# Second-layer row terms of a two-layer graph and expert kernel: broadcast by a trip through DRAM instead of by TensorE

## The chip, the cores and the metric

The kernel runs on one core of a Trainium2 chip. The metric is device time in microseconds (us) of one execution. In the text PE is TensorE (PEld its weight loads), DVE is VectorE, ACT is ScalarE, POOL is GpSimd, and SP is the sync engine, which here only issues DMAs. L525 is line 525 of the kernel before.

## What is computed

The input x holds 64 independent graphs ("batches") of 256 nodes with 256 features; all share one 256x256 adjacency matrix. Two layers follow each other, each a graph attention and a feed-forward part. The change touches the attention of the second layer:

```
h = layernorm(x) @ W                     # L1_gnn
e_src, e_dst = h @ a[:256], h @ a[256:]
e = leaky_relu(e_src[:, :, None] + e_dst[:, None, :], 0.01)
e = where(adj == 0, -1e9, e)
x = x + relu(softmax(e, -1) @ h)
```

Its feed-forward part sends every node to two of eight experts (256 to 256 to 256, with gelu) and adds the weighted results.

## The kernel before

**Work and order.** Each batch of 256 rows is two tiles of 128 rows. The function `batch_layers` is a generator for one batch: it records some instructions and then yields a number. The main loop at the end of the kernel runs in steps; three steps (TICKS) after one batch a new one begins, so that about seven batches are in flight. In a step every live generator runs once, in the order of the numbers they yielded (a lower number first); a positive number ends the generator's turn until the next step, a negative one puts it back into the same step with that rank. The order so recorded is the order of each engine's instructions; every engine and every DMA queue works strictly in its order. Expert work (`expert_pair`, pairs of 128 rows of one expert) is put between the batches' pieces by the same ranks.

**The second layer's scores.** After exponentials, leaky_relu turns into a maximum: for a target node j and a source node i the unnormalised weight is me[j, i] times max(term[i], own[j]). `projected1` (L513) has ACT write three numbers per node into the small tile `ex`: a factor that goes into the masked matrix `me` (L519), the row term, and the node's own term. The row terms lie one to a partition, but the scores need all 256 of them along the free axis in every partition. `scores1` makes this with two PE transposes of a broadcast column (L525) into a PSUM bank named `pd`, and then DVE computes the two halves of the score tile `z1` (L530) with `scalar_tensor_tensor`. `z1` has one buffer, 128 x 2 x 256 float32. In a later step `attended` (L586) multiplies `z1` with the projected nodes on PE (the 128x257 form of that line), and ACT takes out the result (L690).

**The first layer does the same by DMA.** From batch 1 on, `send_terms` (L539) collects the first layer's terms with a DVE transpose, a 4 KB DMA writes them to DRAM (L623), and a second DMA, `spread_terms` (L556), reads them into all 128 partitions of the last part of the score tile `z4`, 512 KB. From batch 18 (SETTLED) on both are issued on SP, before that on ACT.

**SP's queue.** In a step in the middle SP issues, in this order: the first layer's terms to DRAM (L623, waits for DVE), the next batch's input (L96, 256 KB, named `xin`), the spread of the terms (L556, waits until L623 has landed), the store of an earlier batch's result (L736), then for two expert pairs the rows (L893, four DMAs), the row tails (L904) and the weights (L922), and the next batch's blocks (L106, four DMAs).

PSUM is eight banks used in turn (tag "bank"), whatever they hold. POOL sends rows to the experts' regions (L1061) and adds expert results to the output (L991) by indirect DMAs.

Of the kernel before, what the change touches and what calls it, by code (L numbers as in the profile page):

```python
# [9 lines left out]
F32 = mybir.dt.float32  # L10
I32 = mybir.dt.int32
AF = mybir.ActivationFunctionType
ALU = mybir.AluOpType
AX = mybir.AxisListType

P = 128
# [5 lines left out]
def rows_to_all(ap: bass.AP, n: int) -> bass.AP:  # L22

    return bass.AP(tensor=ap.tensor, offset=ap.offset, ap=[[0, P], [1, n]])
# [3 lines left out]
def kernel(  # L28
# [17 lines left out]
    nc = tc.nc  # L46
    B, N, D = x.shape
# [4 lines left out]
    NT = N // P  # L52
# [21 lines left out]
    work = ctx.enter_context(tc.tile_pool(name="work", bufs=2))  # L74
# [4 lines left out]
    def bank(name, shape):  # L79
        t = psum.tile([P, 2 * D], F32, tag="bank", name=name, bufs=8)  # L80
        n = 1
        for s in shape:
            n *= s
        t = t[:, :n]
        if len(shape) == 2:
            t = t.rearrange("p (a b) -> p a b", a=shape[0])
        elif len(shape) == 3:
            t = t.rearrange("p (a b c) -> p a b c", a=shape[0], b=shape[1])
        return t
# [39 lines left out]
    SETTLED = CHUNKS[0] + CHUNKS[1] + CHUNKS[2] + CHUNKS[3] + 2  # L129


    ident = const.tile([P, P], F32, tag="ident", name="ident")
# [191 lines left out]
    def once(work):  # L324
# [14 lines left out]
        out=tri, in_=tri, pattern=[[1, P]], base=0, channel_multiplier=-1,  # L339
# [154 lines left out]
    for i in range(2):  # L494
        t = keep.tile([P, NT, D + 1], F32, tag=f"q1_{i}", name=f"q1_{i}")
# [3 lines left out]
    def projected1(xT, rstd, b):  # L499

        q = q1s[b % 2]
        pqs = []
        for t in range(NT):
            pq = bank("pq", [D + 3])
            for k in range(KT):
                nc.tensor.matmul(  # L506
                    pq, xT[:, k, t * P : (t + 1) * P], wx1[:, k, :],
                    start=(k == 0), stop=(k == KT - 1),
                )
            pqs.append(pq)  # L510
        ex = small.tile([P, NT, 3], F32, tag="ex1", name="ex1")
        for t, pq in enumerate(pqs):
            nc.scalar.activation(ex[:, t, :], pq[:, D:], AF.Exp, scale=rstd[:, t : t + 1])  # L513
            nc.scalar.activation(
                q[:, t, :D], pq[:, :D], AF.Copy, scale=rstd[:, t : t + 1]
            )
        me = work.tile([P, NT, N], F32, tag="me", name="me", bufs=1)
        for j in range(NT):
            nc.scalar.activation(me[:, j, :], masks[1][:, j, :], AF.Copy, scale=ex[:, j, 0:1])  # L519
        return q, ex, me  # L520

    def scores1(ex, me):
        pd = bank("pd", [N])
        for t in range(NT):
            nc.tensor.transpose(  # L525
                pd[:, t * P : (t + 1) * P], ex[:, t, 1:2].to_broadcast([P, P]), ident
            )
        z = work.tile([P, NT, N], F32, tag="z1", name="z1", bufs=1)
        for j in range(NT):
            nc.vector.scalar_tensor_tensor(  # L530
                z[:, j, :], pd, ex[:, j, 2:3], me[:, j, :], op0=ALU.max, op1=ALU.mult
            )
        return [z[:, j, :] for j in range(NT)]

    def send_terms(q, b):


        ut = small.tile([P, S], F32, tag="ut", name="ut", bufs=1)
        nc.vector.transpose(  # L539
            ut.rearrange("p (t h w) -> p t h w", t=NT, h=H), q[:, :, :, HD - 1 : HD + 3]  # L540
        )
        ud = tc.dram_tile([S, S], F32, name=f"terms_{b}")
        ud = ud.rearrange("c r -> (c r)").rearrange("(c p) -> c p", p=P)
        return ut, ud
# [51 lines left out]
    def batch_layers(b, c0, xng, lg):  # L596
# [23 lines left out]
        if b:  # L620
            ut, ud = send_terms(q, b)
            yield -31
            terms_queue(b).dma_start(  # L623
                out=ud.rearrange("c (g r) -> g c r", g=G),
                in_=ut[2 : P : S // (NT * H), :],
            )
            yield -52
        z = work.tile([P, NT, NT, H, P], F32, tag="z4", name="z4", bufs=2)
# [17 lines left out]
        ex = work.tile([P, NT, D], F32, tag="e", name="e", bufs=1)  # L646
# [21 lines left out]
        for t in range(NT):  # L668
            nc.vector.scalar_tensor_tensor(  # L669
                x2[:, t, :], pf[:, t, :], rstd[:, t : t + 1], x1b[:, t, :],  # L670
                op0=ALU.mult, op1=ALU.add, accum_out=sums[:, t : t + 1],
# [6 lines left out]
        xT = transposed(x2)  # L678
        yield 20
        q, ex, me = projected1(xT, rstd, b)  # L680
        yield 25
        z = scores1(ex, me)
        yield 40
        pvs, rinv = attended(
            q[:, :, None, :], 1, lambda j, h, t: z[j][:, t * P : (t + 1) * P]
# [9 lines left out]
        for t in range(NT):  # L695
            nc.vector.scalar_tensor_tensor(
                x2[:, t, :], x2[:, t, :], 1.0, rel[:, t, :],
                op0=ALU.mult, op1=ALU.add, accum_out=sums[:, t : t + 1],
# [36 lines left out]
        if not dense:  # L735
            d = nc.sync.dma_start(  # L736
                out=out_rows[b * N : (b + 1) * N, :].rearrange("(t p) d -> p t d", p=P), in_=base
# [476 lines left out]
    def jobs():  # L1214
        b = done = taken = 0
        for c, nb in enumerate(CHUNKS + (1,) * DENSE):
            nt = nb * NT
            lg = keep.tile([P, nt, E], F32, tag="lg", name=f"lg_{c}", bufs=7)
            xng = []
            row0 = b * N  # L1220
            done += nt
            n = max(done - (E - 1) - taken, 0) if b < ROUTED else 0
            taken += n
            for i in range(nb):
                def job(b=b, c=c, i=i, nb=nb, nt=nt, n=n, lg=lg, xng=xng, row0=row0):
                    yield from batch_layers(b, i * NT, xng, lg)
                    if i == nb - 1:
                        if b >= ROUTED:
                            yield 65
                            yield from route_dense(b, lg)  # L1230
                        else:
                            yield from route(c, row0, nt, n, b == ROUTED - 1, xng, lg)
                yield job()
                b += 1
# [85 lines left out]
```

## Time and profile before

| | us |
|---|---|
| median of 3 runs (1497.18 to 1500.99) | 1497.51 |
| the profiled execution, its own time | 1509.41 |
| its span, first to last instruction | 1507.6 |
| PE busy in the span | 1429.0 (95%) |
| DVE busy | 1252.7 (83%) |
| ACT busy | 1024.6 (68%) |
| POOL busy | 870.2 (58%) |

The span of the profiled execution is 1.8 us shorter than its own time, and that time is 11.9 us (0.8%) above the median of the runs; differences are therefore made against the profiled execution and then put onto the median. The mean granted clock of PE was 0.986. The span has three stretches: some 300 us in which the pipeline of batches fills and the first experts begin, a steady part up to about 1300 us with a new batch every 20.3 us, and an end of about 200 us in which only expert work is left. The row of L525 (128 transposes, 26.1 us busy) and that of L530 (128 instructions, 53.8 us busy) are those of the scores concerned.

### The profile page before, as it was taken

What the parts mean: (1) busy time and instruction counts of PE and PEld (TensorE: products, weight loads), DVE (VectorE), ACT (ScalarE), POOL (GpSimd) and SP (SyncE); (2) the same over time, 40 slices, a digit from 0 to 9 for tenths busy, and PEclk for the clock granted to TensorE, in tenths of its full rate; (3) what the DMA queues carried; (4) which work ended last, traced back from release to release, by engine and by line L of the source; (5) the groups of instructions that cost most, each with busy time, mean ns of one, the idle gap of its engine ahead of it and who ended that gap; (6) DMA issues with size and microseconds to landing.
All of it is one profiled execution on the core that took longest, in us unless ns stands there. A gap on an engine that the chain in (4) does not pass through costs nothing. (4 is left out here: it accounts for less than half of the span.)

```text
span 1507.6 us, 30029 instructions
## 1 busy us (share of the span) xinstructions
PE 1429.0 (95%) x8138; PEld 1263.9 (84%) x8138; DVE 1252.7 (83%) x4476; ACT 1024.6 (68%) x2403; POOL 870.2 (58%) x845
## 2 busy tenths in 40 slices
PE   6899999999999999999999999999999999879996
PEld 5788888889898998988998989888888887658885
DVE  7699999888898888889898988998888888765543
ACT  1477667577777777777777787667777878764331
POOL 2122536355867576666758585776666667643444
PEclk9899999899999999999999999999999999999999
DMA  4732334556877777877877677768777775887843
GB/s 134 241 97 67 117 104 131 155 149 142 196 172 190 157 183 155 177 177 180 187 157 183 151 186 164 181 164 187 179 167 170 153 170 124 192 180 161 156 83 50
DMA packets 354354, 236.37 MB, mean 157 GB/s; under 512 B 246276, under 2 KB 316428, under 8 KB 354188
## 3 DMA queue, kind: packets, MB, share of 16 engines
q1 hardware_dynamic: 301272, 158.16, 41.3%
q0 software_dynamic: 48864, 66.33, 23.8%
q10 hardware_dynamic: 4052, 9.98, 2.2%
q8 instruction: 67, 1.10, 0.3%
q14 instruction: 99, 0.81, 0.2%
HBM read 146.00 MB, written 88.35 MB: 155 GB/s over the span
## 5 line engine op out<-in xcount | busy, mean ns | idle before, releaser
L991 POOL DMA_INDIRECT out_dram<-y,xt x258 | 414.1, 1605 | 206.6 <-issue 71.5
L586 PE MATMUL pv<-q,z 128*128 128x65 f32 (+1 forms) x2560 | 365.9, 298 | 0.4
L586 PEld LDWEIGHTS pv<-q,z 128*128 128x128 f32 x2560 | 333.0, 194 | 13.1 <-DVE z L572 1.1
L1061 POOL DMA_INDIRECT xs<-xng,pos x244 | 259.5, 1064 | 65.3 <-issue 60.3
L970 PE MATMUL py<-w2s,hT 128*128 (+1 forms) x1224 | 283.5, 382 | 11.5 <-ACT hT L961 10.3
L970 PEld LDWEIGHTS py<-w2s,hT 128*128 128x128 f32 x1224 | 229.1, 191 | 45.4 <-ACT hT L961 14.2
L955 PE MATMUL ph<-sT,we 128*128 128x256 f32 x1032 | 241.9, 383 | 4.5 <-DVE y L980 2.9
L572 DVE SCALAR_TENSOR_TENSOR z<-z,q,mask 128x256 f32<-128x256 f32 x504 | 231.6, 482 | 15.5 <-DMA z<-terms 6.6
L955 PEld LDWEIGHTS ph<-sT,we 128*128 128x128 f32 x1032 | 195.6, 192 | 32.4 <-DVE y L980 3.6
L461 ACT COPY xT<-pt 128x512 f32<-128x512 f32 x209 | 121.4, 588 | 105.0 <-PE pt L455 72.2
L948 ACT ACTIVATE y<-y,w 128x256 f32<-128x256 f32 x258 | 113.2, 498 | 115.3 <-DVE y L980 100.9
L961 ACT ACTIVATE hT<-ph,we 128x256 f32<-128x256 f32 x306 | 124.1, 472 | 63.5 <-PE ph L955 46.3
L408 POOL TENSOR_SCALAR rstd<-mv 128x4 f32<-128x4 f32 (+1 forms) x66 | 15.6, 236 | 239.4 <-DVE mv L381 184.4
L506 PE MATMUL pq<-wx,xT 128*128 128x259 f32 x512 | 128.8, 394 | 18.6 <-ACT xT L461 16.9
L426 ACT ACTIVATE off<-x,sums 128x256 f32<-128x256 f32 x256 | 129.3, 505 | 8.4 <-DVE x L669 1.6
L506 PEld LDWEIGHTS pq<-wx,xT 128*128 128x128 f32 x512 | 95.6, 193 | 42.6 <-ACT xT L461 25.6
L471 PE MATMUL pq<-wx,xT 128*128 128x268 f32 x512 | 127.1, 391 | 2.8 <-DVE xT L117 1.6
L980 DVE TENSOR_TENSOR y<-py,b2s 128x512 f32<-128x512 f32 x129 | 85.7, 685 | 50.0 <-PE py L970 37.3
L662 PE MATMUL pf<-wfT,xT 128*128 128x256 f32 x512 | 123.8, 385 | 0.0
L471 PEld LDWEIGHTS pq<-wx,xT 128*128 128x128 f32 x512 | 97.5, 191 | 21.9 <-DVE xT L117 1.8
L690 ACT ACTIVATE rel<-pv,rinv 128x256 f32<-128x256 f32 x128 | 54.0, 469 | 76.4 <-DVE rinv L593 52.2
L662 PEld LDWEIGHTS pf<-wfT,xT 128*128 128x128 f32 x512 | 94.7, 195 | 10.8
(174 smaller groups left out, 2400.8 us busy)
## 6 DMA issues: line engine op xcount, KB each, us to landing
we<-wpack SPq DMA_DIRECT2D x145, 288.0 KB
xr<-xs SPq DMA_DIRECT2D x516, 64.0 KB
z<-terms SPq DMA_DIRECT2D x46, 512.0 KB
xin<-in_x_dram SPq DMA_DIRECT2D x64, 256.0 KB
out_dram<-base SPq DMA_DIRECT2D x61, 256.0 KB
xblk<-in_x_dram SPq DMA_DIRECT2D x188, 64.0 KB
z<-terms ACTq DMA_DIRECT2D x17, 512.0 KB
out_dram<-y,xt POOLq DMA_INDIRECT x258
```

Source lines behind the costliest of these rows:

```text
L426: nc.scalar.activation(off, src[:, t, :], AF.Square, bias=sums[:, t : t + 1], scale=-float(D), accum_out=sq[:, at + t : at + t + 1],)
L461: nc.scalar.copy(dst, pt)
L471: nc.tensor.matmul(pq.rearrange("p h c -> p (h c)"), xT[:, k, t * P : (t + 1) * P], wx[:, k, :], start=(k == 0), stop=(k == KT - 1),)
L506: nc.tensor.matmul(pq, xT[:, k, t * P : (t + 1) * P], wx1[:, k, :], start=(k == 0), stop=(k == KT - 1),)
L572: nc.vector.scalar_tensor_tensor(z[:, j, :, h, :], terms, q[:, j, h, HD + 2 : HD + 3], masks[0][:, j, :].rearrange("p (t i) -> p t i", t=N ...
L586: nc.tensor.matmul(pv[:, h, :], z(j, h, t), q[:, j, h, : d + 1], start=(j == 0), stop=(j == NT - 1),)
L662: nc.tensor.matmul(pf[:, t, :], xT[:, k, t * P : (t + 1) * P], wfT[:, k, :], start=(k == 0), stop=(k == KT - 1),)
L955: nc.tensor.matmul(ph[:, f, :], we[:, k * D + f * P : k * D + (f + 1) * P], xT[:, k, :], start=(k == 0), stop=(k == KT - 1),)
L961: nc.scalar.activation(hT[:, f, :], ph[:, f, :], AF.Gelu, bias=we[:, C_B1 + f : C_B1 + f + 1])
L970: nc.tensor.matmul(py[:, t, :], hT[:, f, t * P : (t + 1) * P], w2s[:, e, f * D : (f + 1) * D].rearrange("p e c -> p (e c)"), start=(f == 0 ...
L991: d = nc.gpsimd.indirect_dma_start(out=out_rows, out_offset=bass.IndirectOffsetOnAxis(ap=xt[:, t, 0:1].bitcast(I32), axis=0), in_=y[:, t, ...
L1061: d = nc.gpsimd.indirect_dma_start(out=xs_d[: E * CAP * PAIR, :], out_offset=bass.IndirectOffsetOnAxis(ap=at, axis=0), in_=xe, in_offset=None,
```

## The change

For batches 18 to 63 (46 of 64) the second layer's row terms no longer go over PE. In the step that computes `ex`, a DMA on SP writes the 256 terms out of `ex` into a DRAM tile (`send_terms1`, 256 pieces of 4 bytes); later in the same step a second DMA on SP reads them into all 128 partitions of the second half of `z1` (128 pieces of 1 KB, 128 KB). `scores1` takes its terms from there: the first half of the scores is written beside them, the second half over them. `z1` is therefore taken one step earlier than before. The rank of `scores1` in its step goes from 25 to 45. Batches 0 to 17 keep the transposes.

In the built program the order of DVE, ACT and POOL is unchanged; PE's is unchanged but for the 92 transposes that are gone; SP's is unchanged but for 92 DMAs that are added. In the middle of the program the write of the second layer's terms stands just ahead of L623, and the read just behind `xin` (L96) and just ahead of L556. For the last seven batches no `xin` stands between; for the last three, which have no first-layer terms beside them, the read stands right behind its write.

```diff
-    def scores1(ex, me):
-        pd = bank("pd", [N])
-        for t in range(NT):
-            nc.tensor.transpose(
-                pd[:, t * P : (t + 1) * P], ex[:, t, 1:2].to_broadcast([P, P]), ident
-            )
-        z = work.tile([P, NT, N], F32, tag="z1", name="z1", bufs=1)
+    def send_terms1(ex, b):
+
+        ud = tc.dram_tile([N], F32, name=f"terms1_{b}")
+        nc.sync.dma_start(out=ud.rearrange("(t p) -> p t", p=P), in_=ex[:, :, 1])
+        return ud
+
+    def scores1(ex, me, z, spread):
+
+        terms = z[:, NT - 1, :]
+        if not spread:
+            terms = bank("pd", [N])
+            for t in range(NT):
+                nc.tensor.transpose(
+                    terms[:, t * P : (t + 1) * P], ex[:, t, 1:2].to_broadcast([P, P]), ident
+                )
         for j in range(NT):
             nc.vector.scalar_tensor_tensor(
-                z[:, j, :], pd, ex[:, j, 2:3], me[:, j, :], op0=ALU.max, op1=ALU.mult
+                z[:, j, :], terms, ex[:, j, 2:3], me[:, j, :], op0=ALU.max, op1=ALU.mult
             )
...
         q, ex, me = projected1(xT, rstd, b)
-        yield 25
-        z = scores1(ex, me)
+        spread = b >= SETTLED
+        if spread:
+            yield -22
+            ud = send_terms1(ex, b)
+            yield -52
+        z = work.tile([P, NT, N], F32, tag="z1", name="z1", bufs=1)
+        if spread:
+            nc.sync.dma_start(out=z[:, NT - 1, :], in_=rows_to_all(ud, N))
+        yield 45 if spread else 25
+        z = scores1(ex, me, z, spread)
         yield 40
```

## The prediction

> **What bounds the kernel now.** I read the page's first part, then the busy times of stretches, then the timeline of one batch engine by engine, then PE's and SP's waits. PE leads, and the stretches say where:
>
> ```profile
> 320.00:960.00 640.00, 633.16 (x3739) 569.07 (x3738) 569.46 (x1968) 483.02 (x1142) 430.19 (x405) 1.00 0.75 172
> 960.00:1310.00 350.00, 328.40 (x1826) 287.83 (x1825) 302.15 (x1210) 271.41 (x590) 235.87 (x218) 0.98 0.76 167
> ```
>
> Columns: stretch and length, then busy us of PE, PEld, DVE, ACT, POOL, then clock, DMA share, GB/s. From 320 to 960 us (batches 18 to 48) PE is busy 99% of the time, DVE 89%. From 960 to 1310 (batches 49 to 63) PE is busy 94%, DVE 86%. PE's waits in the first stretch are 6.6 us of 640, for one cause:
>
> ```profile
> PE pq L506 <- ACT xT L461: 6.2, 8, 1.3
> PE pq L506 <- issue: 0.4, 1, 0.4
> ```
>
> So up to 960 us the end is PE's own work, and what PE issues less is saved. Later it is PE with some stalls (7.5 us there for DVE's x of L669, 6.9 us for ACT's xT).
>
> **What the Trainium skill says.** (1) "Perfetto Trace Analysis", Identifying the Most-Contended Engine: matmul busy time misleads because matmuls are pipelined. It does here: a transpose of L525 lasts 273 ns on the page, but PE goes on after 109. (2) "TensorE: Matmul & The Clock Gate", Part 4: a 128x128 transpose took about 275 ns in a kernel, most of it SBUF access latency; the 273 ns agree. (3) "DMA: Bandwidth & Descriptors", Anatomy of one DMA: about 2.0 us fixed, mostly the receipt of the write, plus bytes / 436 GB/s. The trace agrees: L556, which waits for L623 to land, is issued 2.24 us or less after it (below). (4) "VectorE: DVE Perf Modes", The TRN2 errata: a source in PSUM costs a DVE instruction 120 fixed cycles, one in SBUF 58. The trace does not: L572 from SBUF takes 483 ns (median), the 128x256 instructions from the PSUM bank 470 to 473. The measurement decides.
>
> **What is removed: 92 transposes.** The end of one batch's transposes in PE's timeline:
>
> ```profile
> 817.97 3.62 PE L970 MATMUL py<-w2s,hT 128*128 x16
> 821.42 0.38 PE L525 MATMUL pd<-ident,ex 128*128 128x128 f32 x2
> 821.64 1.56 PE L586 MATMUL pv<-q,z 128*128 128x65 f32 x13
> ```
>
> From start to start the two take 821.64 - 821.42 = 0.22 us; the 273 ns overlap with what follows. Batches 18 to 48: 31 x 0.22 = 6.8 us, with PE saturated, all on the path. Batches 49 to 63: 15 x 0.22 = 3.3 us, plus PE's waits for `ex` ahead of L525 and its weight load, 2.2 us in that stretch; I take half, 1.1, as what follows is sometimes late too. Sum 11.2 us; ends: 6.8 (nothing from the later stretch) and 12.3. The freed PSUM bank can only make later banks free earlier; I cost it at nothing, since PE shows no wait for a bank in the steady stretch.
>
> **What is added: two DMAs a batch on SP.** SP's timeline of the same batch, after ACT's `ex` and before DVE's scores (three views):
>
> ```profile
> 817.17 0.27 ACT L513 ACTIVATE ex<-pq,rstd 128x3 f32<-128x3 f32 x1
> ```
> ```profile
> 819.94 0.54 SPq L623 DMA_DIRECT2D terms<-ut  x1
> 820.52 0.45 SPq L96 DMA_DIRECT2D xin<-in_x_dram  x1
> 822.18 0.35 SPq L556 DMA_DIRECT2D z<-terms  x1
> ```
> ```profile
> 824.94 0.83 DVE L530 SCALAR_TENSOR_TENSOR z<-pd,ex,me 128x256 f32<-128x256 f32 x2
> 825.69 0.17 DVE L593 RECIPROCAL rinv<-pv 128x4 f32<-128x4 f32 x1
> 826.28 0.18 DVE L593 RECIPROCAL rinv<-pv 128x4 f32<-128x4 f32 x1 [0.42 <-PE pt L455]
> ```
>
> *The write.* It can go at 817.5, when `ex` is done; SP is idle there, since its next instruction, L623, waits for DVE until 819.94. Issue 0.39 (xt of L904, also 256 pieces) to 0.55 us (L623): hidden. Landing: like L623's, 1.7 to 2.2 us, as the lower end; no row shows 256 stores of 4 bytes, so 4 us as the upper. Thus landed at 819.2 to 821.5.
>
> *The read.* It stands behind xin, whose issue ends at 820.97, and ahead of L556, which waits until 822.18 anyway. It can go at 821.1 and takes some 0.35 us of issue: hidden in the 1.2 us. (With the slow write it goes at 821.5 and may hold L556 by a few tenths; L556's data are needed 8 us later or more, so that costs nothing.) Its buffer is free: the matmuls of the batch before that read `z1` were issued from 811.60 on, for 1.9 us. Landing: at least the fixed 2.0 plus 128 KB at 436 GB/s, 2.3 us. At most, with xin's 256 KB ahead: 393,000 bytes at 172 GB/s / 0.75 = 229 GB/s (the stretch's rate over its share), 1.7 us, so 3.7. (The fixed part and the 436 are estimates from the DMA page.) It lands at 823.4 to 824.8; I take 824.2. DVE wants it at 824.94, so it is on time by 0.1 to 1.5 us. Over the steady batches DVE gets to L530 3.1 to 4.3 us after the end of xin's issue; the shortest third may be late by some tenths. Behind L530 in DVE's order stand the reciprocals of L593, the product of L641 and x2 of L669, for which PE's transposes wait. But the second L593 waits for PE by 0.42 us here: that covers a small lateness. Cost up to 960 us: 0; upper end 31 x 0.3 = 9 us.
>
> *Later batches.* Here the margin is smaller. At 1058.12 xin is issued (0.45 us), at 1060.94 DVE reaches L530: 2.4 us instead of 3.1 to 4.3, and the same order holds for about ten batches. Against a landing of 2.3 to 3.7 us after 1058.7 DVE waits 0 to 1.4 us, say 0.6. PE is ahead of DVE there: it next needs DVE's x2 (finished at 1064.5) only after pl, issued from 1066.20 for 0.95 us. So I charge a third: 10 x 0.6 / 3 = 2 us; ends 0 and 14. For the last three the read follows its write directly, two landings (4 to 5 us) after `ex`: batch 61 has 4.4 us (1255.54 to 1259.96), the others more: a few tenths once. SP also stands still for 2 us there, behind which expert loads wait (batch 63: four us later than now); five row buffers are loaded ahead, cost 0, upper end 4.
>
> *SP itself.* 0.9 us more issue a batch. It waits long each batch ahead of L623:
>
> ```profile
> SPq L623 <- DVE stats L380: 343.7, 45, 11.4
> SPq L556 <- DMA terms<-ut: 41.1, 45, 2.2
> ```
>
> 343.7 / 45 = 7.6 us idle: hidden. *DMA engines:* 46 x 128 KB over some 1000 us are 6 GB/s beside 170, and 384 packets a batch: cost 0, as the queue's other loads have steps in hand; it is inside the landing's upper end. *DVE:* terms from SBUF, 483 - 470 = 13 ns x 92 = 1.2 us, hidden in the wait at L593. *Ranks:* 25 to 45 changes no engine's order.
>
> **Sum.** -11.2 + 2 = -9.2 us. The profiled time 1509.4 would become 1500.2, and the median, which stands 11.9 us lower, 1497.5 - 9.2 = 1488.3; I say 1488.
>
> **Rivals.**
> A. As summed, PE's issue time is what goes: 1485.5 to 1492. Chance 0.63. For it: PE at 99%.
> B. It all comes off, and earlier banks and fewer stalls give a little more: -13 or more, 1484.5. 0.11.
> C. The later part swallows it: only 6.8 us are saved, and ten or twelve late reads cost DVE, and through it PE, their full 0.6 us: 6.8 - 6.6 = about 0, 1494 to 1500. For it: DVE's gaps are few after 960 us. Against: PE's lead of 1 to 2 us over DVE there. 0.14.
> D. Slower: the read queued behind xin lands late in every batch. It decides from about 4.5 us after its issue on: margin 3 to 4 plus the 0.4 us of L593. At 5 us (L893's second group is let go only when L556's 512 KB have landed, some 5 us after their issue, so this length does occur) DVE stands 0.5 to 1 us in 46 batches: +23 to 46 us, less 11: 1509 to 1532. Against: 128 KB are a quarter of those 512. 0.09.
> E. A change without effect, the DMAs costing what PE saves by chance: within 0.3%, in C's range. 0.03.
>
> **How the numbers follow.** A measurement of this kernel tells some 0.3%, 4.5 us, from no change. Faster by more: A and B, and a small part of C: 0.76. Same: most of C and E: 0.14. Slower: D and the tail of C: 0.10. The range holds A, B and half of C: 1484 to 1498.
>
> **What would show it in the profile after.** 36 transposes of L525's kind instead of 128; PE's stretch of a batch 0.22 us shorter, the pace from 320 us on 20.1 instead of 20.3 us; DVE's wait for "z from terms", now 6.6 us in all, up by under 10 us, in the late batches; SP's wait ahead of the write short. I am wrong if DVE's wait for the terms grows beyond 20 us, if PE's idle time grows by what its work shrinks, or if expert loads come late at the end.

## The result and the profile after

| | before | after |
|---|---|---|
| median of 6 runs each, us | 1497.35 | 1822.76 |
| span of the profiled execution, us | 1507.6 | 1816.8 |
| PE busy, us | 1429.0 (95%) | 1527.7 (84%) |
| mean granted clock of PE | 0.986 | 0.910 |

The changed kernel is slower: ratio 1.217, 95% interval 1.214 to 1.220, some 325 us. The forecast of 1488 us was wrong in size and in sign.

In the kernel after, what was L530 is L538, L556 is L564, L623 is L631, L641 is L649, L647 is L655, L669 is L677. The new write is L525, the new read L696. The same stretches, cut so that they hold about the same batches as the two shown of before (columns as there):

```profile
320.00:1160.00 840.00, 695.42 (x3679) 605.08 (x3677) 571.70 (x1963) 483.18 (x1137) 428.65 (x406) 0.90 0.71 137
1160.00:1620.00 460.00, 360.70 (x1816) 313.57 (x1816) 307.12 (x1216) 273.31 (x595) 241.97 (x220) 0.87 0.67 129
```

In the first stretch DVE's 1963 instructions cost 572 us, as the 1968 of before did (569). But they take 840 us of time instead of 640: the work is the same, and 200 us of standing are added. PE was busy 99% and is now busy 83%, at a clock of 0.90 instead of 1.00. The waits of all engines (us in total, times, longest us) say who stands first:

```profile
DVE z L538 <- DMA z<-terms: 322.3, 46, 10.0
ACT e L655 <- DVE hp L649: 278.9, 44, 9.7
POOL rstd L446 <- ACT off L426: 240.8, 53, 11.2
...
PEld pt L455 <- DVE x L677: 213.1, 82, 9.8
PE pt L455 <- DVE x L677: 199.5, 55, 9.4
```

In the same list of before the four lower ones stood so (L641 and L669 are DVE's lines there):

```profile
POOL rstd L446 <- ACT off L426: 98.5, 33, 4.6
...
ACT e L647 <- DVE hp L641: 21.0, 30, 3.1
PEld pt L455 <- DVE x L669: 19.5, 28, 4.8
...
PE pt L455 <- DVE x L669: 13.4, 10, 4.4
```

Of the five after only DVE's is a wait for a DMA, in each of the 46 batches, 322.3 / 46 = 7.0 us each time. The growth of the others is what stands behind it: L649 and L677 come after L538 in DVE's order, and ACT's L426 works on the x of L677. The group row of L538 carries the same number (busy, mean ns of one, idle before it):

```profile
L538 DVE SCALAR_TENSOR_TENSOR z<-z,ex,me 128x256 f32<-128x256 f32 x92 | 44.6, 484 | 324.2 <-DMA z<-terms 322.3
```

Which of the two DMAs is late is in SP's timeline of one batch (start, duration, line), and in DVE's and PE's of the same time:

```profile
1003.47 0.38 SPq L525 DMA_DIRECT2D terms<-ex  x1
1005.95 0.55 SPq L631 DMA_DIRECT2D terms<-ut  x1
1006.55 1.87 SPq L96 DMA_DIRECT2D xin<-in_x_dram  x1
1012.53 0.34 SPq L696 DMA_DIRECT2D z<-terms  x1
1012.97 0.46 SPq L564 DMA_DIRECT2D z<-terms  x1
```
```profile
1009.27 1.31 DVE L117 STREAM_TRANSPOSE sT<-xr 128x512 f32<-128x512 f32 x2
1018.26 1.00 DVE L538 SCALAR_TENSOR_TENSOR z<-z,ex,me 128x256 f32<-128x256 f32 x2 [7.68 <-DMA z<-terms]
1019.18 0.24 DVE L601 RECIPROCAL rinv<-pv 128x4 f32<-128x4 f32 x2
```
```profile
1016.08 0.95 PE L766 MATMUL pl<-rT,xT 128*128 128x8 f32 x8
1021.29 1.12 PE L455 MATMUL pt<-ident,x 128*128 128x128 f32 x4 [4.26 <-DVE x L677]
```

The write is issued at 1003.47, the read at 1012.53: SP stood ahead of the read until the write had landed, 9.1 us. The read takes 5.7 us more. DVE was at L538 at 1010.58 and stands 7.68 us, and PE 4.26 us behind it. SP's own waits repeat this for the whole program:

```profile
SPq L525 <- ACT q L514: 276.3, 46, 15.3
SPq L696 <- DMA terms<-ex: 242.0, 45, 9.4
```

A DMA tells that it is done by increments of a semaphore, and whoever needs its data waits for them. In the trace a DMA counts as landed with the last of its increments. Medians over the 46 batches, from issue to landing, in us (for `xin` over the 39 loads that are issued behind the new write, and the same 39 of before):

| | before | after |
|---|---|---|
| write of 256 terms of 4 B (L525) | - | 9.03 (7.60 to 11.30) |
| read of 128 x 1 KB (L696) | - | 5.22 |
| write of the first layer's terms, 4 KB (L623, now L631) | 1.67 | 7.22 |
| `xin`, 256 KB (L96) | 2.78 | 8.38 |
| spread of 512 KB (L556, now L564) | 4.74 | 5.77 |

The trace of before holds only some of the 16 increments of most reads of this kind (7 in the median for L556), so 4.74 may be too low, and a growth to 5.77 is not shown.

In one such write that I followed (issued at 869.76), all 256 packets were under way within 2 us of its issue, nearly all of 9 ns, but its 16 increments arrived from 1.96 to 8.15 us. So nothing is long in transfer; the increments come late, and the two DMAs issued behind the write land late with it.

### The profile page after: what moved, and what is told of

It is laid out like the page before. It is cut to its first block, busy times and chain, and to the rows that moved or that the text cites. A ratio compares the mean times of both kernels' runs of the same rounds, so it can differ in the third digit from the quotient of the medians.

```text
span 1816.8 us, 30001 instructions
## 1 busy us (share of the span) xinstructions
PE 1527.7 (84%) x8046; PEld 1329.2 (73%) x8046; DVE 1259.2 (69%) x4476; ACT 1026.4 (56%) x2403; POOL 872.1 (48%) x845
## 5 line engine op out<-in xcount | busy, mean ns | idle before, releaser
L594 PE MATMUL pv<-q,z 128*128 128x65 f32 (+1 forms) x2560 | 421.3, 324 | 5.6 <-DVE z L538 4.5
L594 PEld LDWEIGHTS pv<-q,z 128*128 128x128 f32 x2560 | 373.3, 210 | 33.4 <-issue 4.6
L538 DVE SCALAR_TENSOR_TENSOR z<-z,ex,me 128x256 f32<-128x256 f32 x92 | 44.6, 484 | 324.2 <-DMA z<-terms 322.3
L455 PE MATMUL pt<-ident,x 128*128 128x128 f32 x512 | 101.2, 322 | 199.5 <-DVE x L677 199.5
L971 PE MATMUL ph<-sT,we 128*128 128x256 f32 x1032 | 252.7, 396 | 1.4 <-DVE sT L117 0.8
L580 DVE SCALAR_TENSOR_TENSOR z<-z,q,mask 128x256 f32<-128x256 f32 x504 | 231.5, 482 | 15.7 <-DMA z<-terms 6.7
L455 PEld LDWEIGHTS pt<-ident,x 128*128 128x128 f32 x512 | 64.8, 158 | 224.8 <-DVE x L677 213.1
L655 ACT ACTIVATE e<-hp 128x512 f32<-128x512 f32 x64 | 40.3, 630 | 305.0 <-DVE hp L649 278.9
L506 PE MATMUL pq<-wx,xT 128*128 128x259 f32 x512 | 139.3, 419 | 47.0 <-ACT xT L461 46.9
L506 PEld LDWEIGHTS pq<-wx,xT 128*128 128x128 f32 x512 | 101.8, 206 | 79.8 <-ACT xT L461 64.2
L446 POOL TENSOR_SCALAR rstd<-sq 128x4 f32<-128x4 f32 (+1 forms) x63 | 21.8, 347 | 241.5 <-ACT off L426 240.8
L426 ACT ACTIVATE off<-x,sums 128x256 f32<-128x256 f32 x256 | 129.3, 505 | 9.9 <-DVE x L677 3.6
```

Source lines behind the costliest of these rows:

```text
L426: nc.scalar.activation(off, src[:, t, :], AF.Square, bias=sums[:, t : t + 1], scale=-float(D), accum_out=sq[:, at + t : at + t + 1],)
L455: nc.tensor.transpose(pt[:, k, t * P : (t + 1) * P], by_block(src[:, t, :])[:, k] if blocks else src[:, t, k * P : (k + 1) * P], ident,)
L506: nc.tensor.matmul(pq, xT[:, k, t * P : (t + 1) * P], wx1[:, k, :], start=(k == 0), stop=(k == KT - 1),)
L580: nc.vector.scalar_tensor_tensor(z[:, j, :, h, :], terms, q[:, j, h, HD + 2 : HD + 3], masks[0][:, j, :].rearrange("p (t i) -> p t i", t=N ...
L594: nc.tensor.matmul(pv[:, h, :], z(j, h, t), q[:, j, h, : d + 1], start=(j == 0), stop=(j == NT - 1),)
L971: nc.tensor.matmul(ph[:, f, :], we[:, k * D + f * P : k * D + (f + 1) * P], xT[:, k, :], start=(k == 0), stop=(k == KT - 1),)
```

## The experiments

Ratios are against the kernel before, run on the same chip; 1.003 is about 4.5 us. "Neighbours" are the 4-byte pieces as the change writes them, side by side in DRAM.

My theory after the result: **neighbouring small pieces are confirmed one after another (same place)**. Rivals: **it is the 4-byte piece as such**, wherever it goes; **it is the read** behind xin (rival D); **it is SP's queue**, whatever its DMAs do.

### Write alone, read alone

*Write alone.* The terms are written, nobody reads them, the transposes stay on PE.

```diff
-        spread = b >= SETTLED
-        if spread:
+        spread = False
+        if b >= SETTLED:
             yield -22
-            ud = send_terms1(ex, b)
-            yield -52
+            send_terms1(ex, b)
...
-        if spread:
-            nc.sync.dma_start(out=z[:, NT - 1, :], in_=rows_to_all(ud, N))
-        yield 45 if spread else 25
+        yield 25
```

> The write of 256 pieces of 4 bytes is issued for batches 18 to 63 as in the changed kernel, nobody reads it, and the transposes stay on PE. Latency theory (what costs is that DVE stands for data that come late; the write itself takes 8 to 9 us from issue to landing): the write still lands after 7 to 9 us, the first layer's 4 KB write behind it after 6 to 8, but nobody needs them in time, so the kernel takes 1495 to 1515 us. Clogging theory (the small writes hold up every other transfer, and that is what costs): 1550 us or more, with waits for expert rows and inputs.

Measured 1.082 (1.077 to 1.086), about 122 us, for a write that no engine waits for. It lands after 9.74 us, `terms<-ut` after 8.60, `xin` after 9.34. SP's waits and then all engines':

```profile
SPq L564 <- DMA terms<-ut: 298.1, 42, 10.5
```
```profile
POOL out_dram L1004 <- DMA out_dram<-y,xt: 126.7, 30, 11.0
...
DVE z L580 <- DMA z<-terms: 77.6, 32, 7.0
```

Before, the spread was issued some 2 us after the first layer's terms; now SP waits 298.1 / 42 = 7.1 us for L631 to land, and with it the spread, the rows and the weights behind it are late. DVE's wait for the spread (L580 here) was 6.6 us before.

Nor is SP's queue alone hit. POOL's wait for its own DMAs into the output was smaller before:

```profile
POOL out_dram L991 <- DMA out_dram<-y,xt: 32.1, 9, 6.2
```

Of these DMAs, the 56 whose issue ended within 5 us after a write of terms landed 8.7 us later in the median, the 198 others of the same part of the run 3.4 us. In the changed kernel it is 9.1 us (30) against 3.6 (225). With the terms written 64 bytes apart (below) it is 2.4 (42) against 3.1 (212).

So the write does harm twice: to its own reader, and to other DMAs that run beside or behind it. The expectation of 1495 to 1515 us, which knew only the first, fails; the other one, of 1550 us or more, came true.

*Read alone.* The read takes a DRAM tile that is filled once with ones; no write, no transposes.

```diff
+    terms_d = tc.dram_tile([N], F32, name="terms1")
...
-        ud = tc.dram_tile([N], F32, name=f"terms1_{b}")
-        nc.sync.dma_start(out=ud.rearrange("(t p) -> p t", p=P), in_=ex[:, :, 1])
-        return ud
+        return terms_d
```

> The read into all partitions stays where it is in the changed kernel, but from a DRAM tile filled once with ones; no write in the batches and no transposes from batch 18 on, so the second layer's scores there use ones as row terms. Latency theory with the write as cause: DVE's wait for z from terms falls from 322 us to under 25 us, and the kernel takes 1487 to 1505 us. If the read by itself is late (it landed 5.2 us after its issue in the changed kernel, against a margin of 3 to 4 us): DVE waits 1 to 2 us a batch, 46 to 90 us in all, and the kernel takes 1530 to 1590 us.

Measured 1.0165 (1.009 to 1.024). The read lands after 4.38 us and DVE waits 0.9 us on average in 35 batches:

```profile
DVE z L540 <- DMA z<-terms: 31.4, 35, 2.0
```

Time and wait lie between the two expectations. The read is not the 325 us, but it is late by itself, and that alone turns the hoped gain into a loss of 25 us.

### Is it the piece or the place?

*512 bytes apart.* 256 pieces of 4 bytes again, each at the start of its own 512 bytes. In this run and the next four all batches share one DRAM tile, filled with ones once, and the read takes its first 1 KB, so the terms are not the right ones.

```diff
+    terms_d = tc.dram_tile([N, P], F32, name="terms1")
...
-        nc.sync.dma_start(out=ud.rearrange("(t p) -> p t", p=P), in_=ex[:, :, 1])
+        nc.sync.dma_start(
+            out=terms_d.rearrange("(t p) c -> p t c", p=P)[:, :, 0], in_=ex[:, :, 1]
+        )
...
```

> As the changed kernel, still 256 pieces of 4 bytes a batch, but written 512 bytes apart into one DRAM tile that all batches share and that was filled with ones once; the read takes the first 1 KB of that tile, so most row terms are ones. It waits for the write as before. Theory of the same place (the writes fall into the same 1 KB of DRAM and are acknowledged one after the other, 24 ns each): the write lands after 2 to 4 us and the kernel takes 1490 to 1560 us. Theory of the piece (each small write costs that much wherever it goes): it lands after 8 to 9 us and the kernel takes 1800 to 1840 us.

*Half the pieces,* neighbours: only the first tile's 128 terms are written.

```diff
+    terms_d = tc.dram_tile([N], F32, name="terms1")
...
+        nc.sync.dma_start(
+            out=terms_d.rearrange("(t p) -> p t", p=P)[:, 0:1], in_=ex[:, 0:1, 1]
+        )
...
```

> As the changed kernel, but only the first tile's 128 terms are written (128 pieces of 4 bytes, neighbours in DRAM); the other 128 terms are ones. If the landing time grows with the number of pieces (2 us and 24 to 28 ns a piece): it lands after 5 to 5.5 us, DVE's wait falls from 7.0 to 3 to 4 us a batch, and the kernel takes 1620 to 1690 us. If a small write costs a fixed time whatever the number: 8 to 9 us and 1800 us or more.

*Thirty-two pieces,* neighbours: the same with `[:S, 0:1]` on both sides, S = 32.

> As the changed kernel, but only 32 terms of the first tile are written, 32 pieces of 4 bytes that are neighbours in 128 bytes of DRAM; the other terms are ones. Half the pieces (128) had landed as late as all 256 (9.0 us in the median). If writes wait for one another within a small unit of DRAM (64 bytes, 16 pieces, about 0.4 us each), different units side by side: it lands after 7 to 9 us still, and the kernel takes 1700 us or more. If they wait within each 512 bytes (128 pieces, about 55 ns each): 32 pieces land after 3 to 4.5 us, and the kernel takes 1530 to 1620 us.

*64 and 16 bytes apart.* As with 512 bytes, with a tile of `[N, 16]` or `[N, 4]` numbers.

> The 256 pieces of 4 bytes go into one shared DRAM tile again, but 64 bytes apart (a tile of 256 x 16 numbers) instead of 512 bytes apart; the read takes the tile's first 1 KB, so the terms are not the right ones. Known: 512 bytes apart the write lands after 2.1 us, as neighbours after 9.0, 32 neighbours alone after 5.0. Theory U512 (pieces that share a stretch of 512 bytes follow one another, other stretches go on beside it): 8 pieces share a stretch, so about a quarter of what 32 add (3.3 us): landing 2.5 to 3.3 us, time near the 512-byte spacing, 1.020 to 1.035. Theory U64 (only pieces within 64 bytes follow one another): landing 2.0 to 2.2 us, 1.018 to 1.025. Theory N (what counts is the number of small pieces in one region of many KB): 7 us or more, 1.15 to 1.20.

> The same with the pieces 16 bytes apart (a tile of 256 x 4 numbers, 4 KB). Theory U512: 32 pieces share a stretch of 512 bytes, as many as in the run with 32 neighbours alone, so landing near 5 us, time 1.06 to 1.10. Theory U64: 4 pieces share 64 bytes, a quarter of what 16 neighbours share: landing 2.5 to 4 us if the 16 neighbours of each 64 bytes are what made 9.0, 1.02 to 1.06. Theory N: 7 us or more, 1.15 to 1.20.

| write of 4-byte pieces | lands after, us | DVE's wait for the terms, us | ratio (95%) |
|---|---|---|---|
| 256 neighbours (after) | 9.03 | 322.3 | 1.217 (1.214 to 1.220) |
| 128 neighbours | 8.98 | 297.2 | 1.199 (1.194 to 1.205) |
| 32 neighbours | 4.97 | 131.2 | 1.082 (1.077 to 1.086) |
| 256, 16 bytes apart | 2.98 | 44.1 | 1.019 (1.016 to 1.021) |
| 256, 64 bytes apart | 2.08 | 40.5 | 1.017 (1.015 to 1.020) |
| 256, 512 bytes apart | 2.07 | 35.5 | 1.020 (1.016 to 1.025) |
| no write (read alone) | - | 31.4 | 1.016 (1.009 to 1.024) |

The wait of DVE in all engines' waits, and SP's wait ahead of the read, for the run with 64 bytes between pieces:

```profile
DVE z L543 <- DMA z<-terms: 40.5, 43, 2.2
```
```profile
SPq L701 <- DMA terms<-ex: 2.6, 2, 2.2
```

The same number of pieces of the same size on the same queue: 9.0 us side by side, 2.1 us when 64 bytes apart. The piece as such and the queue are out; what is shown is that it depends on the place. The shared tile is not the reason: 128 neighbours in such a tile are as slow as 256 in a tile of their own. With the pieces apart nothing is left but the read's own lateness. Closer than 64 bytes it begins (no distance between 16 and 64 was run): at 16 bytes, 4 pieces in 64 bytes, 0.9 us are added. That fits "only within 64 bytes" of the expectations, not the stretch of 512 bytes and not the count of pieces; the ratios of the two runs lie just below the ranges given. One thing doesn't fit: 32 and 128 neighbours are equally dense, but take 5.0 and 9.0 us, while 128 and 256 take the same. So the expectation for half the pieces (5 to 5.5 us) failed, and that for 32 was met on neither side (7 to 9 or 3 to 4.5). Why 32 are quicker than 128 stays open, and that the pieces are confirmed one after another is the theory's picture, which no trace shows.

### The read: 128 readers of one place

*128 rows.* The read alone again, but each partition reads a 1 KB row of its own instead of the same 1 KB.

```diff
+    terms_d = tc.dram_tile([P, N], F32, name="terms1")
...
-            nc.sync.dma_start(out=z[:, NT - 1, :], in_=rows_to_all(ud, N))
+            nc.sync.dma_start(out=z[:, NT - 1, :], in_=ud)
```

> As the run with the read alone, but the read takes 128 different rows of 1 KB of a DRAM tile filled once with ones (131 KB) instead of the same 1 KB 128 times; row terms from batch 18 on are ones. If the read landed late (4.4 us in the median) because all partitions read the same place: it lands after 3 us or less, DVE's wait falls from 31 us to under 10 us, and the kernel takes 1487 to 1500 us. If it is late for its size and for what stands ahead of it in the queue: it lands after 4 to 4.5 us and the kernel takes 1515 to 1530 us.

Measured 0.9994 (0.9976 to 1.0011). The read lands after 2.36 us instead of 4.38, with the same bytes, packets and neighbours in the queue. (This trace holds few of the increments, three of 16 in the median, so 2.36 may be too low; the four reads with all 16 took 2.1 to 3.6.) DVE's group row of the scores now (idle before it behind the last bar):

```profile
L540 DVE SCALAR_TENSOR_TENSOR z<-z,ex,me 128x256 f32<-128x256 f32 x92 | 43.3, 471 | 7.2 <-DMA z<-terms 3.1 <-issue 2.1
```

3.1 us of waiting instead of 31.4. So the read too is late mainly because of its place. What xin ahead of it adds is smaller; the runs below with the read ahead of xin show about half a microsecond.

*Nothing in place of the transposes.* No write, no read; the scores take any tile for their terms. This measures what is there to be gained.

```diff
-        terms = z[:, NT - 1, :]
+        terms = masks[0][:, 0, :]
...
-        if spread:
-            yield -22
-            ud = send_terms1(ex, b)
-            yield -52
...
-        if spread:
-            nc.sync.dma_start(out=z[:, NT - 1, :], in_=rows_to_all(ud, N))
```

> From batch 18 on there are neither transposes nor DMAs for the row terms: the scores take a row of the first layer's mask, which lies in SBUF, in place of the terms (so they are not the reference's). What the removal of the 92 transposes is worth by itself: 9 to 12 us by the prediction's own step (0.22 us from start to start, 46 times, and some waits for ex), so 1485 to 1489 us. Rival: PE's time is not what sets the end, and the kernel stays within 4 us of before.

Measured 0.9946 (0.9915 to 0.9978): 8 us, 3 to 13. The first stretch:

```profile
320.00:960.00 640.00, 632.74 (x3713) 570.15 (x3711) 576.07 (x1992) 488.32 (x1154) 435.72 (x408) 1.00 0.77 174
```

Before, PE did 3739 instructions here; less the 31 x 2 transposes, 3677. It now does 3713, 36 more in the same time, worth 36 / 3713 x 640 = 6.2 us. A second measure agrees: from ACT's `ex` (L513) of batch 18 to that of batch 48 the profile of before takes 610.3 us, this one 603.4, 6.9 less. The 6.8 us of the forecast were about right.

### Can the idea be mended?

*Packed.* A DVE transpose gathers the terms into 8 rows of 32, so that the write is 8 pieces of 128 bytes (`ex` becomes 16 numbers wide for it).

```diff
+        ut = small.tile([P, S], F32, tag="ut1", name="ut1", bufs=1)
+        nc.vector.transpose(ut, ex.rearrange("p t c -> p (t c)"))
...
-        nc.sync.dma_start(out=ud.rearrange("(t p) -> p t", p=P), in_=ex[:, :, 1])
+        nc.sync.dma_start(
+            out=ud.rearrange("(t g r) -> g t r", t=NT, g=G), in_=ut[1 : P : S // NT, :]
+        )
```

> As the changed kernel, but DVE first turns the terms with one 32x32-block transpose (0.21 us a batch), so that the write has 8 pieces of 128 bytes instead of 256 of 4; the read stays where it is. Same-place theory: the write lands after 1.6 to 2.7 us as the first layer's does, the kernel comes down to the run with the read alone (1522.6 us) give or take 8 us, with 25 to 40 us of DVE's wait for z from terms left. Theory that any write to DRAM just read back is slow: over 1600 us.

Measured 1.019 (1.016 to 1.022). The write lands after 1.72 us, the read after 4.39, as the read alone does. DVE's wait is a little above the 25 to 40 us expected. All engines' waits:

```profile
DVE z L547 <- DMA z<-terms: 43.4, 39, 2.6
```

*Packed, read ahead of xin* (`yield -52` becomes `-35`):

> As the packed version (DVE transpose, 8 pieces of 128 bytes), but the read stands ahead of the next batch's input (L96) instead of behind it, some 0.5 us earlier in SP's order. Theory of the same place (128 partitions read one 1 KB, 4.4 us, whatever stands ahead): it lands as late after its issue, 4.0 to 4.4 us, and the kernel gains at most the half microsecond a batch: ratio to before 0.998 to 1.012. Theory of the queue (the 256 KB of the input ahead of it delay it): it lands after 3 us or less, and the ratio is 0.993 to 0.998.

Measured 1.006 (1.004 to 1.008), within the range of the theory of the place; the read lands after 3.90 us, just below the 4.0 to 4.4 expected and 0.5 less than behind xin, and DVE's wait halves:

```profile
DVE z L547 <- DMA z<-terms: 21.3, 25, 2.5
```

*Packed, scores and their matmuls one step later* (`yield 99` ahead of the scores; what follows is drawn together so that the batch ends in the same step):

```diff
+        if spread:
+            yield 99
         yield 45 if spread else 25
...
-        yield 60
+        yield -60 if spread else 60
```

> As the packed version, but the scores and the matmuls that use them come one step (6.8 us) later, and the third step of the chain (the sum with the attention's result) is drawn together with the one before it, so that later work keeps its step. Theory of lateness: DVE no longer waits for z from terms (under 5 us in all), and the ratio to before falls from 1.019 to 0.993 to 1.003; what remains above 0.9946 (nothing in place of the transposes) is the DVE transpose and the shorter way behind the scores. If it stays above 1.01, what costs is not DVE's wait for the terms.

Measured 1.021 (1.018 to 1.025), above what was expected. DVE's wait for the second layer's terms is gone; the list shows what came instead:

```profile
PE pq L511 <- ACT xT L461: 46.5, 46, 3.9
...
DVE x L686 <- PE pf L679: 35.3, 47, 2.0
...
DVE rinv L610 <- PE pv L603: 24.5, 39, 1.6
```

With the edit these steps follow one another in one step of the main loop, where a step lay between before: it seems that the later reader is paid for with a shorter way behind it. By its expectation a ratio above 1.01 would mean that DVE's wait is not what costs. As the edit changed both, this run can't decide that; the runs with 128 rows and with 16 copies, which shorten the wait alone, speak for the wait.

*Packed, 16 copies.* The DVE transpose's rows are written to 16 places, 1 KB apart, and each is read by 8 partitions. Once with the read in place, once ahead of xin.

```diff
...
+        ud = tc.dram_tile([16, N], F32, name=f"terms1_{b}")
+        for t in range(NT):
+            nc.sync.dma_start(
+                out=ud.rearrange("c (t g r) -> t g c r", t=NT, g=G)[t],
+                in_=ut[1 + t * S // NT : P : S, None, :].to_broadcast([G, 16, S]),
+            )
...
+            copies = bass.AP(tensor=ud.tensor, offset=ud.offset, ap=[[N, 16], [0, 8], [1, N]])
+            nc.sync.dma_start(
+                out=z[:, NT - 1, :], in_=copies
+            )
```

> As the packed version, but 16 copies of the terms are written (2 DMAs of 64 pieces of 128 bytes, to 16 rows of 1 KB), and each row is read by 8 partitions instead of one row by 128; the read stays behind the next batch's input. Theory of the same place: the read lands after 2.4 to 3.2 us as with 128 different rows, DVE's wait for z from terms falls from 43 us to under 12 us, and the ratio to before is 0.995 to 1.005. If the read's length comes from its size and what is ahead: 4.4 us and a ratio of 1.015 or more.

> The 16 copies and the early read together. If the two lateness terms add: no wait of DVE for these terms is left (under 5 us), and the ratio to before is 0.993 to 1.000, near the run with nothing in place of the transposes (0.9946) plus the DVE transpose of 0.21 us a batch. If DVE's extra instruction or SP's three DMAs a batch now hold things up: 1.003 or more.

In place: 1.011 (1.008 to 1.014), landing after 3.11 us. Ahead of xin: 1.0002 (0.9988 to 1.0016), landing after 2.48 us. The waits of the two:

```profile
DVE z L549 <- DMA z<-terms: 23.4, 22, 4.7
```
```profile
DVE z L549 <- DMA z<-terms: 11.7, 9, 3.2
```

Fewer readers of one place make the read quicker. Both runs missed their expectations in part: in place, 12 us of waiting and 1.005 were the upper ends; ahead of xin, under 5 us of waiting was expected, and the ratio lies at the upper end. The best of these versions is back at the time of before, not below it.

Where the 8 us of the run without terms are lost, the profiles show in part (one profile of each version, so a few us are uncertain; times between ACT's `ex` of the batches named):

| us | batch 18 to 48 | batch 48 to 63 |
|---|---|---|
| before | 610.3 | 360.9 |
| nothing in place of the transposes | 603.4 | 360.7 |
| read alone, 128 rows | 605.4 | 365.1 |
| 16 copies, ahead of xin | 597.8 | 366.7 |

Up to batch 48 the last two are ahead of before; they lose in the batches behind, where the prediction had found the smaller margin. There too lie 11.4 of the 11.7 us that DVE waits for the terms with 16 copies (after 930 us). Why those batches cost the version with 128 rows 4 us, with 2.6 us of waiting there, is not known. Nor was it tried to keep the transposes for the late batches.

## Why the prediction was wrong

- **The step that failed: "Landing: like L623's, 1.7 to 2.2 us, as the lower end; no row shows 256 stores of 4 bytes, so 4 us as the upper."** It measured 9.03. SP stood until then, so the read was issued late, and DVE stood 7.0 us in each batch. L623 was the wrong row to go by: same queue and direction, but pieces of 128 bytes. Pieces of 128 bytes did land after 1.72 us here, and 4-byte pieces 64 bytes apart after 2.08; 256 side by side did not. The upper end of 4 us was not worked out from anything, and the range inherited it. The prediction had said that no row shows this operation; that should have brought a far wider bound, and with it a larger chance for D.
- **"Read landing 2.3 to 3.7 us" was mis-sized.** 2.36 us is right for 128 different rows; 128 readers of one 1 KB took 4.38 alone and 5.22 in the changed kernel. The bounds were bytes and rates. The trace of before had a hint: L556, which also reads one place into all partitions, took 4.74 us or more for 512 KB. The fixed 2.0 us in these bounds is, in the section that the prediction names under (3), a fit for DMAs that GpSimd issues; the prediction put it on SP's DMAs without saying so. On SP the small writes landed sooner, after 1.67 and 1.72 us.
- **"DMA engines: cost 0" failed.** The write alone cost 122 us by delaying other DMAs, POOL's too. The Trainium skill states a mechanism for this, "DMA: Bandwidth & Descriptors", Queues, rings and completion order: a semaphore increment lands only after every earlier write of the same DMA engine, whichever queue it came by. The trace agrees: L631 lands 7.22 us after issue instead of 1.67, `xin` 8.38 instead of 2.78, and POOL's DMAs into the output near a write 9.1 us after theirs, against 3.6 for the others.
- **"SP itself: hidden" is right for the issue (0.38 and 0.34 us) and wrong for the wait.** The prediction had SP reach the read with the terms landed; SP stands there 242.0 / 45 = 5.4 us a batch. Nor is SP's wait ahead of the write short: 276.3 / 46 = 6.0 us, since it comes ahead of L631 now, where SP waited before.
- **The sum.** Of "-11.2 + 2" the first term holds within its ends: the run with no terms measured -8 (-3 to -13), with 6 to 7 of it in the steady stretch against 6.8. In place of the second, +2 for late reads in ten batches, DVE waits 7.0 us in each of 46 batches, 322 us in all, about as much as the 325 us lost. In the runs with other writes, too, the loss is about as large as DVE's wait: 298 us with a wait of 297 (128 neighbours), 125 with 131 (32). PE's clock fell as well, from 0.986 to 0.910; what that costs no run separates.
- **The rivals.** D had the right place (DVE at the scores, every batch, from the margin of 3 to 4 us on) but another cause, the queue behind xin, and a price of 23 to 46 us. With the write mended its size was about right: the packed version costs 1.9%, some 28 us, with a read of 4.39 us. A, B and E took the terms as on time, C as late by 0.6 us in ten or twelve batches. None of the five had a slow write. What C says of the later part, that it takes back what the steady one gains, is seen in the mended versions.
- **What it said would show it wrong** did: DVE's wait for the terms beyond 20 us. It is 322.

## What to carry to other kernels

A DMA's price is not its bytes and its row in the queue alone: look at how its pieces lie in DRAM, on the writing and on the reading side. One number per partition written side by side was the bad case here; numbers gathered into rows of 128 bytes, or written 64 bytes apart, landed soon, and a broadcast came sooner when its readers shared 16 copies. (No run read back terms that lay 64 bytes apart; that would be a read of 4-byte pieces.) Where no row of the profile shows an operation, measure it alone before a critical wait is hung on it, and ask which other DMAs run beside and behind it.

## What the runs showed of the hardware

- 4-byte writes to DRAM: 256 side by side land after 9.03 us, 64 bytes apart after 2.08, 8 pieces of 128 bytes after 1.72. The Trainium skill, "DMA: Bandwidth & Descriptors", Specifications, says that below 512 bytes a DMA engine does a read-modify-write. A price of that for each small piece doesn't show (64 bytes apart is as quick as 512); that neighbours wait for one another would fit it, but no run shows the read.
- While such a slow write is under way other DMAs land late too, though they move other data: on its own queue `xin` after 8.38 us instead of 2.78, on POOL's queue DMAs into the output after 9.1 us instead of 3.6.
- SP's DMAs landed in the order of their issue: of the 1214 with all 16 increments in the trace after, none landed before the one of them issued ahead of it.
- 128 partitions reading one 1 KB row take 4.38 us behind xin and 3.90 ahead of it; 128 rows 2.36 behind it (or somewhat more, see there); 16 copies 3.11 behind it and 2.48 ahead.
- PE standing 199.5 us in 55 pieces for DVE's x went with a lower clock: its mean went from 0.986 to 0.910; PE was busy 99 us longer with 92 instructions fewer.
